# Local attention beside a convolution: softmax divisions moved to GpSimd, one copy per half of the transposed weights, three convolution taps moved off VectorE, both halves scheduled in one group

## The chip, the core and the metric

The kernel runs on one core of a Trainium2 chip, in float32. The metric is device time of one execution in microseconds: 1278.14 us is the median of 3 runs before the change (1277.0 to 1278.47). The profile is of one further execution. PE is TensorE, DVE is VectorE, ACT is ScalarE, POOL is GpSimd; SP issues DMAs.

## The reference, cut to what matters

Three layers follow one another: local attention plus a dynamic convolution, a state-space layer, and a mixture of experts. The change touches the first, on x of shape (2, 256, 48, 48) with 4 heads of 64 channels:

```python
q = (_c1x1(x, Wq, bq) * HD ** (-0.5)).reshape(b * HEAD, HD, n)
k = _c1x1(x, Wk, bk).reshape(b * HEAD, HD, h, w)
v = _c1x1(x, Wv, bv).reshape(b * HEAD, HD, h, w)
uk = _unfold(jnp.pad(k, rpad, mode='reflect'), KA).reshape(b * HEAD, HD, kk, n)   # 7x7 windows
...
att = jnp.einsum('bdn,bdkn->bnk', q, uk + upe[None])
att = jax.nn.softmax(att, axis=-1)
out_att = jnp.einsum('bnk,bdkn->bdn', att, uv).reshape(b, c, h, w)
...
hid = jax.nn.relu(_dwconv(xr, w1))              # depthwise 3x3
oc = _dwconv(hid, w2).reshape(b, kc2, C, h, w)  # depthwise 3x3
...
return rate1 * out_att + rate2 * out_conv
```

Ahead of it stands a group normalisation; the layer's input is added to its output. The kernel adds the convolution's and the attention's part into the tile that holds x.

## The kernel before, in words

Channels lie on partitions, in two halves of 128 (two heads each). The image is cut into blocks of 8 x 16 queries, 18 per batch entry, 36 in all (`block`). The keys that a block can see are 14 x 22 = 308 positions, so its scores are a full 128 x 308 product for each of 4 heads, and a constant mask removes what lies outside a 7 x 7 window. For one half (two heads) of a block:

- `scores` (PE, L776): two products from query tile and key image into a double PSUM bank.
- `least` (DVE, L786): adds the mask, writes the result to the SBUF tile `prob`, and reduces the minimum (queries are scaled by a negative number).
- `exps` (ACT, L797): exponential in place, with the sum read from the accumulator.
- `rden` (DVE, L852): reciprocal of the sums, once per block for all four heads.
- `divide` (ACT, L803): `prob` times the reciprocal, one instruction per head.
- `turn` (PE, L810): six transposes (three pieces of keys for two heads) into a double bank. The pieces are 110, 110 and 88 keys, whole rows of the window.
- `copy` (ACT, L818 and L819): the two long pieces and the short one to the SBUF tile `pt`.
- `mix` (PE, L828): weights times values into a single bank. The values come from a table in HBM by DMA (`val`, SP).
- `add` (DVE, L835): bank plus value bias plus x into x.

The convolution (`convolutions`) works on 8 strips of 24 rows (batch, half, top or bottom). First convolution: tap 4 on ACT (`middle`, L557), taps 1 and 7 as products on ACT into a tile `ct` (L599), added to `hid` by accumulating DMAs that POOL issues (`added`, L603), the other six on DVE (`mac1`, L561). After the ReLU (ACT, L565) the second convolution's nine taps run on DVE (`mac2`, L573), each adding to x in place. Queries (`queries`, L621 and L631), keys (`keys`, with borders copied by POOL at L678 to L685 and a position term by POOL at L654) and values (`values`) are projected as they come due. POOL also scales the next layer's weights in this stage (L428, L449).

The order of instructions is not that of the loops. Each step is given to a planner (`Flow`) with an engine, a cost in ns, what it needs, the buffers it takes and frees, and a due time (`PACE0` per block). Its rank is its due time less the work behind it less a number by kind (`LEAD0`); the planner goes through time and emits, for each free engine, the ready step of lowest rank whose buffers are free. Engines execute in the order emitted, so the planner's costs fix the order, and what really takes longer makes engines wait. POOL's instructions and the DMAs that it issues are kept in that order too. Buffers are counted in `room`: four single and two double PSUM banks, three `prob`, four `pt`, two `ct`, two `hid` and so on.

Of the kernel before, what the change touches and what calls it, by code (L numbers as in the profile page):

```python
# [37 lines left out]
P = 128  # L38
# [3 lines left out]
HD = 64  # L42
# [5 lines left out]
KCH = ((0, 5), (5, 5), (10, 4))  # L48
# [74 lines left out]
class Flow:  # L123
# [8 lines left out]
    def __init__(self, room, lead):  # L132

        self.room, self.lead, self.ops = dict(room), lead, {}
# [8 lines left out]
    @classmethod  # L143
    def kind(cls, key):
        return key if isinstance(key, str) else cls.kind(key[0])

# [3 lines left out]
    def rank(self):  # L150

        after = {k: [] for k in self.ops}
        for k, o in self.ops.items():
            for n in o["needs"]:
                after[n].append(k)
        tail, left = {}, {k: len(after[k]) for k in self.ops}
        ends = [k for k in self.ops if not left[k]]
        for k in ends:
            o = self.ops[k]
            same = [tail[a] for a in after[k] if self.ops[a]["due"] == o["due"]]  # L160
            tail[k] = self.span(o) + max(same, default=0) + self.HOP
            for n in o["needs"]:
                left[n] -= 1
                if not left[n]:
                    ends.append(n)
        return {k: o["due"] - tail[k] - self.lead.get(self.kind(k), 0) for k, o in self.ops.items()}, after
# [62 lines left out]
class Kernel:  # L229
# [49 lines left out]
    def begin_flow(self, pool, room, pace, lead):  # L279

        self.m, self.pace, self.flow, self.tiles, self.last = pool, pace, Flow(room, lead), {}, {}
# [52 lines left out]
    def layer0(self, ctx):  # L334
# [5 lines left out]
        room = dict(bank=4, banks=2, q=2, prob=3, pt=4, val=3, vout=2, hid=2, place=2, ct=2)  # L340
        self.begin_flow(self.pool("att", 1, ctx), room, self.PACE0, self.LEAD0)
        self.kp = [wts.tile([P, HP, HP], F32, name=f"kp{h}") for h in range(NH)]
        self.xp = {(b, h): wts.tile([P, H, W], F32, name=f"xp{b}{h}") for b in range(B) for h in range(NH)}
# [19 lines left out]
    def prepare(self, wts):  # L363
# [15 lines left out]
        for key, cost in (("cst", 9500), ("vec", 9000), ("wp", 8500), ("Wk", 9500), ("Wq", 10500), ("Wv", 11500),  # L379
                          ("win", 22000)):  # L380
            self.arrival((key, 0), cost)
# [7 lines left out]
            new("w2r", NH * 9), v["w2"], r["rate2"], None, ALU.mult), ("vec", 0))  # L389

        self.op(0, ("bv1", 0), "DVE", 220, lambda: vec.tensor_scalar(
            new("bv1", NH), v["bv"], r["rate1"], None, ALU.mult), ("vec", 0))
        self.op(0, ("wv1", 0), "POOL", 1600, lambda: nc.gpsimd.tensor_scalar(
            l0["Wv"], l0["Wv"], r["rate1"], None, ALU.mult), ("vec", 0), ("Wv", 0))
# [63 lines left out]
    def group_norm(self, b):  # L458
# [7 lines left out]
        for h in range(NH):  # L466
# [7 lines left out]
            for i in range(pieces):  # L474
                if i % 2 == 0:
                    self.arrival(("x", (b, h, i // 2)), (4500, 16000)[b] + (i // 2 * NH + h + 1) * 700)
# [50 lines left out]
    def convolutions(self, b):  # L527
# [16 lines left out]
        for n in range(NH * strips):  # L544
# [33 lines left out]
            for k in (1, 7):  # L578
                last = self.added(due, ("1", key, k), rows[0], partial(tap, rows, k=k), hidden, lambda h=h: (self.xp[b, h], 0),
                                  lambda w=w1, k=k: w[:, k : k + 1], before, last)  # L580
            for k in range(9):
                if k != 4 and k not in (1, 7):
# [4 lines left out]
            rest = taps  # L587
            for i, k in enumerate(rest):
                self.op(due, ("c2", (key, k)), "DVE", 1385, partial(mac2, k), *before, uses=[("hid", key)] if i == len(rest) - 1 else [])
                before = [("c2", (key, k))]  # L590

    def added(self, due, key, first, places, out, of, weight, before, last):
# [3 lines left out]
        def product():  # L596
            t = self.large_tile("ct", key, [P, CR + 1, W])
            dst, src = places(o=(t, first), i=of())
            nc.scalar.activation(dst, src, AF.Identity, scale=weight())  # L599

        def issue():
            (dst, _), (t, _) = (places(o=o, i=of()) for o in (out(), (T["ct", key], first)))
            nc.gpsimd.dma_start(dst.rearrange("p r c -> p (r c)"), t.rearrange("p r c -> p (r c)"), accum_op=ALU.add)  # L603

        self.op(due, ("cp", key), "ACT", 1220, product, *before, takes=[("ct", key)])
# [4 lines left out]
    def queries(self, b, rb):  # L610
# [4 lines left out]
        for h in range(NH):  # L615
# [10 lines left out]
            def scale(h=h, key=key):  # L626
                if h == 0:
                    self.large_tile("q", (b, rb), [P, NH, NCB, QR * QC])
                ps = T["bank", ("q", key)][:, : QR * W].rearrange("p (r c) -> p r c", r=QR)
                for cb in range(NCB):  # L630
                    nc.scalar.activation(  # L631
                        T["q", (b, rb)][:, h, cb, :].rearrange("p (r c) -> p r c", r=QR), ps[:, :, cb * QC : (cb + 1) * QC],
                        AF.Identity, bias=l0["bq8"][:, h : h + 1], scale=-(HD ** -0.5),
                    )
# [3 lines left out]
            self.op(c, ("q", key), "ACT", 870, scale, ("qp", key), ("bq8", 0), ("q", (b, rb, 0)) if h else None,  # L638
                    takes=[] if h else [("q", (b, rb))], uses=[("bank", ("q", key))])

    def keys(self, b, g):
# [17 lines left out]
        for h in range(NH):  # L659
# [16 lines left out]
            def border(kp=kp):  # L676
# [4 lines left out]
                for j in range(PAD):  # L681
# [8 lines left out]
                    *[("score", (i, h)) for i in range(old + 1) if b],  # L690
# [64 lines left out]
    def block(self, c):  # L755
# [11 lines left out]
        for h in range(NH):  # L767
            key = (c, h)

            def scores(h=h, key=key):  # L770
                if h == 0:
                    self.large_tile("prob", c, [P, 4, NKEY])
                ps = self.banks_for(("s", key))
                for j in range(2):
# [4 lines left out]
                    )  # L779

# [20 lines left out]
            def divide(h=h):  # L801
                for a in range(2 * h, 2 * h + 2):
                    nc.scalar.mul(T["prob", c][:, a, :], T["prob", c][:, a, :], T["rden", c][:, a : a + 1])  # L803


            def turn(h=h, key=key):
                ps = self.banks_for(("t", key))
                for i, (kr, nr) in enumerate(KCH):
                    for j in range(2):
                        nc.tensor.transpose(  # L810
                            ps[: nr * KC, j, i * P : (i + 1) * P], T["prob", c][:, 2 * h + j, kr * KC : (kr + nr) * KC],
                            self.ident
                        )

            def copy(h=h, key=key):
                full, short = KCH[0][1] * KC, KCH[-1][1] * KC
                pt, ps = self.large_tile("pt", key, [P, 2, len(KCH), P]), T["banks", ("t", key)]
                nc.scalar.copy(pt[:full, :, :2, :].rearrange("p j i q -> p j (i q)"), ps[:full, :, : 2 * P])  # L818
                nc.scalar.copy(pt[:short, :, 2, :], ps[:short, :, 2 * P : 3 * P])  # L819


            def mix(h=h, key=key):
                po = self.bank_for(("o", key))
                for i, (kr, nr) in enumerate(KCH):
                    nk = nr * KC
                    for j in range(2):
                        a = 2 * h + j
                        nc.tensor.matmul(  # L828
                            po[j * HD : (j + 1) * HD, :P], lhsT=T["val", c][:nk, i, a * HD : (a + 1) * HD],
                            rhs=T["pt", key][:nk, j, i, :], start=i == 0, stop=i == len(KCH) - 1,  # L830
                        )

            def add(h=h, key=key):
                x = self.x[b][:, h, :].rearrange("p (r c) -> p r c", r=H)[:, r0 : r0 + QR, c0 : c0 + QC]
                nc.vector.scalar_tensor_tensor(  # L835
                    x, T["bank", ("o", key)][:, :P].rearrange("p (r c) -> p r c", r=QR), self.l0["bv1"][:, h : h + 1],
                    x, ALU.add, ALU.add
                )

            self.op(c, ("score", key), "PE", 512, scores, ("q", (b, rb, h)), *[k for k in rows if k[1][2] == h],  # L840
                    ("score", (c, 0)) if h else None,
                    takes=[("banks", ("s", key))] + ([] if h else [("prob", c)]), mode="rows", uses=[("q", (b, rb))] if last and h == NH - 1 else [])
            self.op(c, ("least", key), "DVE", 950, least, ("score", key), ("cst", 0), ("least", (c, 0)) if h else None,
                    uses=[("banks", ("s", key))])
            self.op(c, ("exps", key), "ACT", 1170, exps, ("least", key), ("exps", (c, 0)) if h else None)
            self.op(c, ("divide", key), "ACT", 990, divide, ("rden", c))
            self.op(c, ("turn", key), "PE", 655, turn, ("divide", key), takes=[("banks", ("t", key))], uses=[("prob", c)])
            self.op(c, ("copy", key), "ACT", 870, copy, ("turn", key), takes=[("pt", key)], uses=[("banks", ("t", key))])
            self.op(c, ("mix", key), "PE", 660, mix, ("copy", key), ("val", c), takes=[("bank", ("o", key))], mode="tiled",
                    uses=[("pt", key)] + ([("val", c)] if h == NH - 1 else []))  # L850
            self.op(c, ("add", key), "DVE", 350, add, ("mix", key), ("bv1", 0), uses=[("bank", ("o", key))])
        self.op(c, ("rden", c), "DVE", 175, lambda: nc.vector.reciprocal(self.small_tile("rden", c, wide), T["den", c]),  # L852
                *[("exps", (c, h)) for h in range(NH)])


        def load():
            val = self.large_tile("val", c, [P, len(KCH), C])
            for i, (kr, nr) in enumerate(KCH):
                nk, first = nr * KC, (r0 + kr) * KC
# [8 lines left out]
        "Wk": -1147950, "Wq": 130187, "Wv": -311640, "add": -66396, "bkp": -1659163, "bq8":  # L868
        487296, "bv1": -67420, "c1": 131452, "c2": -74690, "ca": -343085, "cd": 295831, "copy":
        828342, "cp": -194702, "cst": 1126755, "divide": 116227, "exps": -352759, "ga": 195685,  # L870
        "gneg": 849100, "gs": -87647, "ka": -73324, "kb": -515860, "kk": -132952, "least":
        512500, "line": 1189336, "mix": -72068, "place": -761695, "q": -313065, "qp": -156027,
# [1492 lines left out]
```

## Time and profile before

The profiled execution took 1273.72 us; its span is 1271.9 us.

| engine | busy us in the span | share |
|---|---|---|
| PE | 1210.3 | 95% |
| DVE | 911.8 | 72% |
| ACT | 814.9 | 64% |
| POOL | 574.5 | 45% |

The first layer fills about the first quarter of the span; it is there that DVE and ACT are fullest. In forty slices of 31.8 us:

```profile
PE   4999899997999999999999999999999999999995
...
DVE  6999799997587988789798655655555655556442
ACT  3999899998889888689597653333334343334332
POOL 4723503102267799899889873121212121212220
```

Each digit is a busy share in tenths. A row of groups names line, engine, operation, output and input with their shapes and the count, then the busy time in us and the mean of one in ns, then idle time before the group and who ended it. PE's busy time holds the latency of its pipeline, so a full PE row need not be a full PE.

### The profile page before, as it was taken

The numbers are of one execution on the slowest core, as the hardware profiler recorded it, in microseconds if no ns is written. First come the engines' busy times: TensorE is split into PE (matmuls) and PEld (weight loads), VectorE is DVE, ScalarE is ACT, GpSimd is POOL, SyncE is SP. The second block draws the span as 40 slices with busy tenths as digits, with TensorE's granted clock in tenths as the row PEclk, the third lists the DMA queues.
The fourth block names the chain that finished last, engine by engine and source line by source line (L and its number), as shares of the span: only waits on it lengthen the run. The fifth ranks groups of instructions, "written<-read, shape, count | busy, mean of one in ns | idle before, by whom it ended". The sixth has DMA issues, their size and how long they took to land. (4 is left out here: it accounts for less than half of the span.)

```text
span 1271.9 us, 23413 instructions
## 1 busy us (share of the span) xinstructions
PE 1210.3 (95%) x7952; PEld 966.5 (76%) x7952; DVE 911.8 (72%) x2401; ACT 814.9 (64%) x1978; POOL 574.5 (45%) x781
## 2 busy tenths in 40 slices
PE   4999899997999999999999999999999999999995
PEld 2666566655567777777777888999999999999994
DVE  6999799997587988789798655655555655556442
ACT  3999899998889888689597653333334343334332
POOL 4723503102267799899889873121212121212220
PEclk9999899999899999999999999999999999999998
DMA  8553537241223334334545139667658667656756
GB/s 280 148 148 99 136 113 167 86 106 31 74 87 95 108 99 121 124 103 148 164 144 177 59 134 292 196 229 230 214 171 258 190 229 222 225 172 223 221 177 212
DMA packets 103961, 203.74 MB, mean 160 GB/s; under 512 B 10891, under 2 KB 82908, under 8 KB 98908
## 3 DMA queue, kind: packets, MB, share of 16 engines
q1 hardware_dynamic: 85020, 168.51, 38.5%
q0 software_dynamic: 16704, 29.37, 12.0%
q10 hardware_dynamic: 2116, 4.33, 1.0%
q8 instruction: 65, 1.06, 0.3%
q14 instruction: 56, 0.46, 0.1%
HBM read 154.24 MB, written 43.23 MB: 155 GB/s over the span
## 5 line engine op out<-in xcount | busy, mean ns | idle before, releaser
L2094 POOL DMA_INDIRECT acc<-ey,token x70 | 109.3, 1562 | 367.6 <-ACT ey L2093 324.7
L2088 ACT ACTIVATE hid<-bank,bt 128x256 f32<-128x256 f32 (+1 forms) x288 | 132.0, 460 | 171.0 <-PE bank L2084 166.6
L2084 PE MATMUL bank<-ext,wt 128*128 128x256 f32 (+1 forms) x1152 | 241.3, 368 | 0.0
L2084 PEld LDWEIGHTS bank<-ext,wt 128*128 128x128 f32 x1152 | 207.6, 191 | 24.4
L573 DVE SCALAR_TENSOR_TENSOR x<-hid,w2r,x 128x1128 f32<-128x1128 f32 (+3 forms) x72 | 99.5, 1391 | 4.7 <-ACT hid L565 4.0
L2127 PE MATMUL po<-ts,ss 128*128 128x128 f32 x768 | 96.3, 275 | 0.0
L915 PE MATMUL bank<-xn,win 128*128 128x387 f32 x240 | 92.9, 511 | 2.1 <-ACT t L998 2.1
L1128 DVE SCALAR_TENSOR_TENSOR xc<-bank,vec,xc 128x384 f32<-128x384 f32 x144 | 86.6, 609 | 8.4 <-ACT xc L1117 8.1
L2127 PEld LDWEIGHTS po<-ts,ss 128*128 128x128 f32 x768 | 90.9, 192 | 0.0
L1344 ACT ACTIVATE mt<-mt,cum 128x128 f32<-128x128 f32 x288 | 87.7, 393 | 0.0
L2131 ACT COPY u<-po 128x128 f32<-128x128 f32 x32 | 8.5, 265 | 114.3 <-PE po L2127 114.3
L1678 POOL DMA_INDIRECT xs<-u,rows x72 | 73.3, 1018 | 17.5 <-issue 14.9
L797 ACT ACTIVATE prob<-prob,top 128x308 f32<-128x308 f32 x144 | 79.1, 570 | 0.4 <-DVE top L786 0.4
L1450 PE MATMUL bank<-wout,y 128*128 128x264 f32 x288 | 73.4, 402 | 0.1
L2071 DVE TENSOR_TENSOR ss<-hid 128x512 f32<-128x512 f32 x32 | 22.1, 691 | 70.6 <-ACT hid L2088 70.6
L915 PE MATMUL zbank<-xn,win 128*128 128x384 f32 x192 | 71.2, 493 | 0.0
L803 ACT ACTIVATE prob<-prob,rden 128x308 f32<-128x308 f32 x144 | 68.9, 567 | 1.0 <-DVE rden L852 0.7
L561 DVE SCALAR_TENSOR_TENSOR hid<-xp,vec,hid 128x1175 f32<-128x1175 f32 (+1 forms) x48 | 69.3, 1443 | 0.1
L810 PE MATMUL banks<-cst,prob 128*110 128x128 f32 (+1 forms) x432 | 60.9, 282 | 8.8 <-ACT pt L819 4.1
L810 PEld LDWEIGHTS banks<-cst,prob 128*110 128x110 f32 (+1 forms) x432 | 47.3, 132 | 27.9 <-ACT prob L803 6.9
L786 DVE CUSTOM_DVE_ANT_0 prob<-banks,cst 128x308 f32<-128x308 f32 x144 | 62.0, 471 | 8.9 <-PE banks L776 8.4
L603 POOL DMA_DIRECT2D hid<-ct x16 | 14.1, 884 | 116.3 <-ACT hid L557 88.5
(333 smaller groups left out, 2999.1 us busy)
## 6 DMA issues: line engine op xcount, KB each, us to landing
wt<-in_We SPq DMA_DIRECT2D x36, 2048.0 KB
mt<-decays SPq DMA_DIRECT2D x36, 512.0 KB
ex<-xs SPq DMA_DIRECT2D x36, 265.0 KB
rd<-decays SPq DMA_DIRECT2D x68, 128.0 KB
val<-vtab SPq DMA_DIRECT2D x72, 110.0 KB
bt<-in_We SPq DMA_DIRECT2D x36, 136.0 KB
hid<-ct POOLq DMA_DIRECT2D x8, 600.0 KB, 5.5
hid<-ct POOLq DMA_DIRECT2D x8, 576.0 KB, 5.4
```

Of the source, the lines that this page charges most:

```text
L573: nc.vector.scalar_tensor_tensor(dst, src, w[:, k : k + 1], dst, ALU.mult, ALU.add)
L797: nc.scalar.activation(t, t, AF.Exp, bias=T["top", c][:, a : a + 1], scale=-1.0, accum_out=T["den", c][:, a : a + 1])
L810: nc.tensor.transpose(ps[: nr * KC, j, i * P : (i + 1) * P], T["prob", c][:, 2 * h + j, kr * KC : (kr + nr) * KC], self.ident)
L915: self.nc.tensor.matmul(ps, lhsT=lhs(k), rhs=rhs(k), start=k == 0, stop=k == NH - 1)
L1128: nc.vector.scalar_tensor_tensor(out(), T["bank", ("cv", at)][:, i : i + TB], wc[:, i : i + 1], out(), ALU.mult, ALU.add)
L1344: nc.scalar.activation(t, t, AF.Relu, bias=at_s, scale=-1.0)
L1450: nc.tensor.matmul(ps[:, : C + E], lhsT=T["y", c][:, m, :], rhs=self.l1["wout"][:, m, :], start=m == 0, stop=m == NZ - 1,)
L1678: ins = nc.gpsimd.indirect_dma_start(self.xs, bass.IndirectOffsetOnAxis(ap=of("rows")[:, i, q : q + 1], axis=0), T["u2", g][:, i, :], None,)
L2084: nc.tensor.matmul(ps[:, :rows], lhsT=w1[:, k, c * P : (c + 1) * P], rhs=xt[:, k, :], start=k == 0, stop=k == NH - 1,)
L2088: nc.scalar.activation(hid[:, c, :], ps[:, :rows], AF.Gelu, bias=bt[:, c : c + 1])
L2094: put = nc.gpsimd.indirect_dma_start(self.acc, bass.IndirectOffsetOnAxis(ap=token[:, j : j + 1], axis=0), y, None, compute_op=ALU.add)
L2127: nc.tensor.matmul(p[name], lhsT=v[a][:, c], rhs=v[w][:, c], start=c == 0, stop=c == NHC // 2 - 1)
```

## The change

All of it is in the first layer, but for one new pool of small tiles opened behind it (`self.small = self.pool("small1", 4)`).

- Divisions: the second half of every block and, in every third block, the first half too are scaled by GpSimd (`nc.gpsimd.tensor_scalar`); the rest stay on ACT. The reciprocal is taken per half.
- Pieces of keys: three of nearly equal length (102, 103, 103), so that one ACT copy moves all three.
- Second convolution: tap 4 goes to ACT, into a tile `cg` together with the value bias; taps 1 and 7 go to ACT products and accumulating DMAs into `cg`; DVE adds `cg` to x once per strip and keeps six taps. In the first convolution the DMA taps now come behind the DVE taps, except in the first strip.
- One group: scores of both halves are one planner step, and so are both weighted sums, which share one bank and are added by one DVE instruction.
- Query scaling: one ACT instruction for three blocks instead of three.
- Planner: single banks 4 to 2, double banks 2 to 3, `prob` 3 to 4, two `cg`; leads kept apart for the first and the second batch entry and set anew; arrival times of inputs set later.

```diff
-KCH = ((0, 5), (5, 5), (10, 4))
+KW = -(-NKEY // 3)
+KCH = ((0, NKEY - 2 * KW), (NKEY - 2 * KW, KW), (NKEY - KW, KW))
...
-        room = dict(bank=4, banks=2, q=2, prob=3, pt=4, val=3, vout=2, hid=2, place=2, ct=2)
+        room = dict(bank=2, banks=3, q=2, prob=4, pt=4, val=3, vout=2, hid=2, place=2, ct=2, cg=2)
...
+            before = [last]
+            for k in sorted(set(range(9)) - {4}, key=lambda k: (k in (1, 7)) == (key[:2] == (0, 0))):
+                if k in (1, 7):
+                    last = self.added(due, ("1", key, k), rows, partial(tap, rows, k=k), hidden,
...
-            rest = taps
+            rest = [k for k in taps if k not in (4, 1, 7)]
+            def centre(h=h, top=top, key=key, hidden=hidden):
+                g = self.large_tile("cg", key, [P, CR, W])
+                dst, src = tap((top, top + CR), (g, top), hidden(), 4)
+                nc.scalar.activation(
+                    dst, src, AF.Identity, bias=self.l0["bv1"][:, h : h + 1],
+                    scale=self.l0["w2r"][:, 9 * h + 4 : 9 * h + 5]
+                )
+            def gather(key=key, strip=strip):
+                nc.vector.tensor_add(strip(), strip(), T["cg", key])
+            self.op(due, ("g2", (key, 4)), "ACT", 1200, centre, *before, ("bv1", 0), takes=[("cg", key)], uses=[("hid", key)])
+            last = ("g2", (key, 4))
+            for k in (4, 1, 7):
+                if k != 4:
+                    last = self.added(due, ("2", key, k), (top, top + CR), partial(tap, (top, top + CR), k=k),
+                                      lambda key=key, top=top: (T["cg", key], top), hidden,
...
+            self.op(due, ("c3", key), "DVE", 1290, gather, summed, *before, uses=[("cg", key)])
...
-                for cb in range(NCB):
-                    nc.scalar.activation(
-                        T["q", (b, rb)][:, h, cb, :].rearrange("p (r c) -> p r c", r=QR), ps[:, :, cb * QC : (cb + 1) * QC],
-                        AF.Identity, bias=l0["bq8"][:, h : h + 1], scale=-(HD ** -0.5),
-                    )
+                nc.scalar.activation(
+                    T["q", (b, rb)][:, h].rearrange("p b (r c) -> p b r c", r=QR),
+                    T["bank", ("q", key)][:, : QR * W].rearrange("p (r b c) -> p b r c", r=QR, b=NCB),
+                    AF.Identity, bias=l0["bq8"][:, h : h + 1], scale=-(HD ** -0.5),
+                )
...
+            def inverse(h=h):
+                if ("rden", c) not in T:
+                    self.small_tile("rden", c, wide)
+                part = slice(2 * h, 2 * h + 2)
+                nc.vector.reciprocal(T["rden", c][:, part], T["den", c][:, part])
...
+            def divide(engine, h=h):
                 for a in range(2 * h, 2 * h + 2):
-                    nc.scalar.mul(T["prob", c][:, a, :], T["prob", c][:, a, :], T["rden", c][:, a : a + 1])
+                    t, r = T["prob", c][:, a, :], T["rden", c][:, a : a + 1]
+                    if engine == "ACT":
+                        nc.scalar.mul(t, t, r)
+                    else:
+                        nc.gpsimd.tensor_scalar(t, t, r, None, ALU.mult)
...
-                nc.scalar.copy(pt[:full, :, :2, :].rearrange("p j i q -> p j (i q)"), ps[:full, :, : 2 * P])
-                nc.scalar.copy(pt[:short, :, 2, :], ps[:short, :, 2 * P : 3 * P])
+                nc.scalar.copy(pt[:KW].rearrange("p j i q -> p j (i q)"), ps[:KW, :, : len(KCH) * P])
...
+            engine = "POOL" if h == 1 or c % 3 == 0 else "ACT"
+            self.op(c, ("divide" if engine == "ACT" else "scale", key), engine, 990 if engine == "ACT" else 2650,
+                    partial(divide, engine), ("rden", key))
...
+        self.op(c, ("mix", c), "PE", 1320, mix, *[("copy", (c, h)) for h in range(NH)], ("val", c), takes=[("bank", ("o", c))],
+                mode="tiled", uses=[*[("pt", (c, h)) for h in range(NH)], ("val", c)])
+        def add():
+            x = self.x[b].rearrange("p h (r c) -> p h r c", r=H)[:, :, r0 : r0 + QR, c0 : c0 + QC]
+            po = T["bank", ("o", c)][:, : NH * P].rearrange("p (h r c) -> p h r c", h=NH, r=QR)
+            nc.vector.tensor_add(x, x, po)
```

## The prediction on record

> **What bounds the kernel now.** The whole page says PE 95% busy, but that mixes stages, and its chain that ended last covers only the final 20 us. The change touches the first layer alone (convolution and local attention), so I read the busy times by windows. The edges come from the timeline: the first normalised input is written from 18.3 us on, and the last attention sum ends at 305.75 us, where the next layer's first transposes start.
>
> ```profile
> core 0: us, PE busy (x) PEld busy (x) DVE busy (x) ACT busy (x) POOL busy (x), PEclk, DMA share, GB/s
> ...
> 64.00:128.00 64.00, 61.27 (x451) 39.88 (x449) 62.80 (x128) 62.03 (x172) 17.92 (x45) 1.00 0.45 124
> ...
> 144.00:160.00 16.00, 11.81 (x87) 7.58 (x87) 9.46 (x28) 11.20 (x31) 4.16 (x7) 0.79 0.52 116
> ...
> 18.30:305.75 287.45, 271.83 (x1936) 178.60 (x1936) 268.39 (x566) 268.15 (x706) 83.45 (x178) 0.98 0.47 125
> ```
>
> Read the last row first: in this stage of 287.45 us DVE is busy for 268.4 and ACT for 268.2, both 93%, and both reach 97% in the long windows such as 64 to 128. They bound it together; to shorten the stage both must lose work. POOL does 83.5 and is the free engine. PE's 272 is padded: six transposes alone take 0.84 us and twelve in a row 1.47, so a half block costs PE 0.63, not 0.84; with such steps 72 half blocks of 0.52 + 0.63 + 0.66 us (scores, transposes, weighted sum) need 130 us, and the projections at most the 106 us of their rows: under 240 in all. Two hollow places remain: 144 to 160 us, where ACT stood 4.2 us before a `ct` buffer because an accumulating DMA had not landed, and the tail after 288 us.
>
> The groups by shape, stage rows (count, busy us, mean ns):
>
> ```profile
> L803 ACT ACTIVATE prob<-prob,rden 128x308 f32<-128x308 f32 x144 | 68.9, 567 | 1.0 <-DVE rden L852 0.7
> ...
> L573 DVE SCALAR_TENSOR_TENSOR x<-hid,w2r,x 128x1128 f32<-128x1128 f32 x32 | 44.4, 1388 | 0.2
> L818 ACT COPY pt<-banks 110x512 f32<-110x512 f32 x72 | 42.7, 593 | 6.0 <-PE banks L810 5.1 <-PE bank L828 0.4
> ...
> L819 ACT COPY pt<-banks 88x256 f32<-88x256 f32 x72 | 28.0, 388 | 0.0
> ...
> L835 DVE SCALAR_TENSOR_TENSOR x<-bank,bv,x 128x128 f32<-128x128 f32 x72 | 23.7, 342 | 2.3 <-PE bank L828 1.9
> ```
>
> Consecutive ACT instructions overlap by about 0.09 us and DVE's by 0.08, so I price by what an instruction adds to busy time.
>
> **ACT.** Of 144 divisions 96 go to GpSimd. Four in a row take 1.88 us, 0.47 each: 96 x 0.47 = 45 off. The two copies of a half (0.593 + 0.388, less overlaps 0.80) become one of 768 columns; 256 more columns cost 0.205 us, so 0.593 + 0.205 - 0.09 = 0.71: 72 x 0.09 = 6 off. Three query scalings (72 are 21.0 us busy, so 3 x 0.29) become one of 384 columns; a copy of that size (L1084) takes 0.47, an activation with a bias (L1117) 0.66, and I take 0.57 less 0.09: 24 x 0.4 = 9 off. Added: 8 centre taps and 16 more products, each like the `ct` products of 1.27 us, 24 x 1.18 = 28. Net: 45 + 6 + 9 - 28 = 32 off, ACT 268 to 236. It stops being a bound.
>
> **DVE.** Of 72 second-convolution taps 24 go; the stage's 72 take 99.45 us, 1.38 each: 33.1 off. Added are 8 gathers of 128x1152 from SBUF. Additions of 512 columns (L2070) take 0.69 us, of 1024 (L1352) 1.215, hence 1.35: 10.8 on. The 72 output sums (23.7) become 36 of 256 columns, like an existing sum of that size (L1482: 0.48, less overlap 0.41): 36 x 0.41 = 15, 9 off. 36 reciprocals more at 0.09 to 0.17: 4 on. Net 27 off: 241. The row for the gather is an extrapolation by an eighth, so its error is below 1 us.
>
> **GpSimd.** The changed program's list of instructions holds 96 scalings of 128x308 on POOL, 32 accumulating DMAs instead of 16, and, behind the stage, the same order on all five engines. No row shows a POOL scaling of 308 columns. The one of 256 (L449) takes 0.92 us undisturbed (shortest of four), the one of 512 (L393) 1.60; in between 1.06. But POOL and DVE disturb each other:
>
> ```profile
> 42.96 1.88 POOL L428 TENSOR_SCALAR win<-win,vec 128x640 f32<-128x640 f32 x1
> ...
> 43.23 3.14 DVE L561 SCALAR_TENSOR_TENSOR hid<-xp,vec,hid 128x1128 f32<-128x1128 f32 x2
> ```
>
> ```profile
> 52.04 2.49 POOL L449 TENSOR_SCALAR wout<-wout,vec 128x256 f32<-128x256 f32 x2
> ...
> 52.08 1.67 DVE L561 SCALAR_TENSOR_TENSOR hid<-xp,vec,hid 128x1175 f32<-128x1175 f32 x1
> ...
> 55.16 4.19 DVE L573 SCALAR_TENSOR_TENSOR x<-hid,w2r,x 128x1152 f32<-128x1152 f32 x3
> ...
> 56.70 1.31 POOL L678 COPY kp<-kp 128x10 f32<-128x10 f32 x1
> ```
>
> A ten-column copy, 0.20 us when free, lasts 1.31 when issued into a tap: POOL waits until the tap is over. The other way round DVE loses less: the tap at 52.08, begun behind a 256-column scaling, takes 1.67 instead of 1.43, and the two at 43.23, begun into one of 640 columns, 3.14 instead of 2.7. That is 0.24 and 0.44, as if POOL held DVE only while it reads; for 308 columns I put 0.27.
>
> The Trainium skill ("SBUF — State Buffer", "Who interferes with whom" and the section on the two sides above it) states a rule that speaks against this change: a GpSimd instruction and a DVE instruction with two SBUF inputs take a shared port pair as an exclusive lock for the whole instruction. POOL's waits here fit it; DVE's do not, since 1.88 us of POOL cost a tap 0.44. By the rule DVE would lose up to 96 x 0.55 x 1.06 = 56 us, and the stage would end some 30 us later than before.
>
> Taps and gathers are 96 x 1.4 + 8 x 1.35 = 145 us of DVE's 241, so a POOL reading meets one with a chance of 0.55 to 0.6. DVE's loss: none at best (readings beside work that reads PSUM), 96 x 0.27 = 26 if each hits, and 56 if the whole instruction holds it. I take 96 x 0.55 x 0.27 = 14, nearest to the rows. DVE: 241 + 14 = 255.
>
> A POOL scaling waits for half a tap (0.69) in 0.55 of the cases, 1.06 + 0.38 = 1.44; bounds 1.06 and 1.06 + 1.38 = 2.44. POOL: 83.5 + 96 x 1.44 + 16 x 0.86 (a DMA issue's median) = 235 us, bounds 199 and 331. It covers its work, but barely, in a stage of 270.
>
> The new waits: a half block's transposes now follow reciprocal and POOL instead of reciprocal and ACT, 2.9 us instead of 0.95. Behind them on PE stand other blocks' scores and products; four `prob` tiles instead of three give them room. PSUM is recut (two single banks, three double), which one group for scores and one for the weighted sum need; that can hold PE, whose 240 us leave 30 spare. The 16 added DMAs cost POOL the issues above; each lands 4.8 to 7.7 us later (L603's landings), and three behind one another (product, DMA, DMA, gather) stand beside six taps, 8 us, and other blocks.
>
> **The sum.** DVE is the bound with 255. Before, DVE filled 93.4% of the stage next to an equally full ACT; with ACT at 236 I take 94%: 255 / 0.94 = 271, which is 16 less than 287.45. Start, seam and tail stay inside that share; the tail stays serial, with the last four half blocks' scalings in one row on POOL (4 x 2.1 us). The profiled execution took 1273.7 us (span 1271.9); less 16 it is 1258. It lay 4.4 below the median of 1278.1; on the median I forecast 1262.
>
> **Rivals.**
> 1. DVE loses nothing to POOL: 241 / 0.94 = 256, 31 less, 1247. For it: the minimum with the mask (L786, 144 of 0.47 us) reads PSUM, and POOL's copies beside it stay at 0.2 us. Against: taps follow one another. Chance 0.17.
> 2. POOL becomes the bound, the slower side. It executes in order, scalings queue behind DMA issues that wait for an earlier DMA, and PE, ACT and DVE wait for the scalings. In the profile before, those issues waited 25 us for landings. The stage is longer than now if 83.5 + 13.8 + 25 + 96 s exceeds 287, that is from s = 1.72 us per scaling on. At 1.85: 300 us, 12 more, 1290. For it: most scalings follow a reciprocal, behind which DVE likes to start a tap, and the second of a pair meets the next tap. Against: a scaling that stands ahead of a DMA issue fills time that POOL now spends waiting. Chance 0.18.
> 3. DVE is held for the whole POOL instruction (the 56 us above): (241 + 56) / 0.94 = 316, 1307. The two rows above contradict it. Chance 0.03.
> 4. The work goes, and new waits eat it: twice as many `ct` products, each of which can hold ACT as the one at 151 us did (about 5 us for all engines), and two single banks. Two such stops more, 10 us: 1262 + 10, 1272. Chance 0.15.
> That the change does not do what it says is excluded by the counts above.
>
> **Numbers.** Forecast 1262 (1253 to 1270), chance 0.47; the rivals as given. Range 1245 to 1286: it leaves out rival 3, half of rival 2 and the edge of rival 1. A measurement of this kernel tells 0.2% (2.6 us) from no change. Faster: 0.47 + 0.17 + most of rival 4 = 0.75. Same 0.07: rival 4 with a third or fourth stop, and rival 2 near its turning point. Slower 0.18.
>
> **What would show it.** Right: stage end near 289 us instead of 306; DVE 250 to 260 us busy up to there, ACT near 236, POOL 220 to 250; scalings of 1.2 to 1.7 us; taps beside them lengthened by about 0.3. Wrong: scalings above 1.75 us and PE waiting for POOL (rival 2); taps of 2.4 us beside scalings (rival 3); idle ACT before `ct` (rival 4); a later layer that is not the same length as before.

## The result, and the profile after

The changed kernel takes 1531.43 us (median of 4 runs, 1528.0 to 1532.38) beside 1278.31 for the kernel before in the same job (4 runs, 1277.0 to 1282.81): ratio 1.197, 95% interval [1.193, 1.200]. The prediction had 1262 with a range of 1245 to 1286. It is wrong in sign, and by 269 us in size.

Where the 253 us lie is quickly found. The last attention sum ends at 560.3 us instead of 305.75; what follows it takes 970.0 us of the span instead of 966.15. The first layer has become 255 us longer. The forty slices, 38.3 us each now:

```profile
PE   4755376546575549999999999989999999999996
...
DVE  7733274434453416888888898546555555565552
ACT  2734283535373428988878887623343333433333
POOL 5823172325353323678989989851222222222221
PEclk9967697767786759999999999999999999999998
```

In the first fourteen slices no engine is full, and TensorE's granted clock has fallen too. The stage by windows (columns as in the prediction):

```profile
18.30:560.30 542.00, 324.22 (x1936) 223.54 (x1935) 243.34 (x548) 244.70 (x513) 222.38 (x291) 0.75 0.33 83
```

The work did go as planned: DVE 243 us (268 before), ACT 245 (268), GpSimd 222 (83). PE's 324 us belong to the same 1936 products as the 272 before; with the clock at 0.75 and gaps between them, each counts for more. With 542 us to fill, all of this is under 60%. Such a stage may well wait for something that is no engine. The groups of the stage by shape:

```profile
L853 POOL TENSOR_SCALAR prob<-prob,rden 128x308 f32<-128x308 f32 x96 | 140.6, 1646 | 191.1 <-DVE rden L845 176.6 <-PE banks L810 14.4
...
L865 ACT COPY pt<-banks 103x768 f32<-103x768 f32 x72 | 55.9, 798 | 91.2 <-PE banks L859 55.5 <-PE bank L885 35.5
...
L577 DVE SCALAR_TENSOR_TENSOR x<-hid,w2r,x 128x1128 f32<-128x1128 f32 x32 | 46.0, 1438 | 0.5
...
L896 DVE TENSOR_TENSOR x<-x,bank 128x256 f32<-128x256 f32 x36 | 15.1, 419 | 185.5 <-PE bank L885 185.3
```

Busy times and means are about as planned; the idle times before the groups (third part) are new. The output sums (L896) take 15 us, and DVE stands still before them for 185. The waits (engine, line, releaser: us in all, times, longest; PEld is TensorE's loading of weights):

```profile
DVE x L896 <- PE bank L885: 185.3, 26, 17.2
POOL prob L853 <- DVE rden L845: 176.6, 16, 32.0
PEld bank L885 <- DMA val<-vtab: 159.3, 40, 9.9
PE bank L885 <- DMA val<-vtab: 156.4, 40, 9.6
ACT vout L755 <- DMA vraster<-vout: 83.4, 4, 24.4
```

Read from the bottom up: the first two rows are engines waiting for engines, which explains nothing yet; in the last three a DMA is late. L885 is the weighted sum, `val` its values from HBM. Its wait (156 us) and that of the value projection for its own copy to HBM (83 us, same SP queue) make 240 us, about the 255 that are missing, though the two may overlap in part. In the stage of the kernel before, neither wait shows at all.

A stretch of the timeline with the loads (start, duration, engine, line, operation, tile, count, idle time before and releaser):

```profile
500.91 0.44 PE L885 MATMUL bank<-pt,val 103*64 103x128 f32 x4 [0.34 <-DMA val<-vtab]
505.45 2.04 PE L885 MATMUL bank<-pt,val 103*64 103x128 f32 x20 [4.10 <-DMA val<-vtab]
510.91 0.70 PE L885 MATMUL bank<-pt,val 103*64 103x128 f32 x4 [3.42 <-DMA val<-vtab]
515.43 1.97 PE L885 MATMUL bank<-pt,val 103*64 103x128 f32 x16 [3.82 <-DMA val<-vtab]
```

and what the DMA engines moved from 500 to 530 us, in slices of 0.75 us:

```profile
DMA  2300000000000131000000000013100599910010
GB/s 55 101 31 23 23 23 22 23 23 23 22 23 23 41 108 36 23 23 23 22 23 23 23 22 23 23 40 83 61 23 23 112 198 235 241 33 15 15 36 13
```

PE starts a new piece every 4.5 us, and between them the chip moves a steady 23 GB/s with 16 DMA engines almost idle (0 tenths). 103 KB in 4.5 us are 23 GB/s: one load is under way, on what looks like one engine of 16. SP, which issues the loads, is now held by most of the issues themselves (SPq is SP's queue of instructions; duration in ns: least, median, longest). The first row is from the kernel after, the second from the kernel before:

```profile
L904 SPq DMA_DIRECT2D val<-vtab x108: 260/4435/9547, 64.4 to 543.0; - x108
```

```profile
L860 SPq DMA_DIRECT2D val<-vtab x108: 282/356/1645, 62.3 to 294.2; - x108
```

Added up, these 108 issues hold SP for 354 us (48 before), most of the stage of 542, and the value projection's copies to HBM are issued by SP in between. The two long loads of a block, at 4.5 us each, need 330 us for 36 blocks; how the rest of the 542 is made up was not taken apart.

The long loads carry fewer bytes than before, 103 KB instead of 110. What changed is the number of partitions, 103 instead of 110. The Trainium skill ("DMA: Bandwidth & Descriptors", "Why a DMA increments its semaphore by 16 and not by 1") states that a transfer is spread over the largest number of engines up to 16 that divides the size of the slowest dimension on both its sides. By that rule 110 rows go to 11 engines, 88 to 11, 102 to 6, and 103, a prime, to one. The trace agrees with one engine for 103. The same page ("Specifications") gives about 27 GiB/s for an engine, which is 29 GB/s. Here 23 GB/s were measured, and the measurement decides.

### The profile page after: what moved, and what is told of

It reads as the page before. It is cut to its first block, busy times and chain, and to the rows that moved or that the text cites. A ratio compares the mean times of both kernels' runs of the same rounds, so it can differ in the third digit from the quotient of the medians.

```text
span 1530.3 us, 23342 instructions
## 1 busy us (share of the span) xinstructions
PE 1263.7 (83%) x7952; PEld 1011.5 (66%) x7952; DVE 890.8 (58%) x2385; ACT 793.3 (52%) x1786; POOL 713.5 (47%) x893
## 5 line engine op out<-in xcount | busy, mean ns | idle before, releaser
L853 POOL TENSOR_SCALAR prob<-prob,rden 128x308 f32<-128x308 f32 x96 | 140.6, 1646 | 191.1 <-DVE rden L845 176.6
L885 PE MATMUL bank<-pt,val 103*64 103x128 f32 (+1 forms) x864 | 87.7, 354 | 157.8 <-DMA val<-vtab 156.4
L885 PEld LDWEIGHTS bank<-pt,val 103*64 103x64 f32 (+1 forms) x864 | 63.7, 178 | 179.4 <-DMA val<-vtab 159.3
L896 DVE TENSOR_TENSOR x<-x,bank 128x256 f32<-128x256 f32 x36 | 15.1, 419 | 185.5 <-PE bank L885 185.3
L865 ACT COPY pt<-banks 103x768 f32<-103x768 f32 x72 | 55.9, 798 | 91.2 <-PE banks L859 55.5
L859 PE MATMUL banks<-cst,prob 128*103 128x128 f32 x432 | 72.0, 320 | 25.7 <-ACT pt L865 21.4
L859 PEld LDWEIGHTS banks<-cst,prob 128*103 128x103 f32 x432 | 63.0, 203 | 42.5 <-ACT pt L865 21.3
L810 PE MATMUL banks<-kp,q 64*128 64x308 f32 x288 | 58.2, 526 | 19.2 <-ACT pt L865 16.1
L1501 PE MATMUL bank<-wout,y 128*128 128x264 f32 x288 | 70.3, 389 | 0.1
```

The lines of the kernel that those rows point to most:

```text
L853: nc.gpsimd.tensor_scalar(t, t, r, None, ALU.mult)
L859: nc.tensor.transpose(ps[:KW, j, i * P : (i + 1) * P], T["prob", c][:, 2 * h + j, k0 : k0 + KW], self.ident)
L885: nc.tensor.matmul(po[j * HD : (j + 1) * HD, h * P : (h + 1) * P], lhsT=T["val", c][:nk, i, a * HD : (a + 1) * HD], rhs=T["pt", (c, h)][:n ...
```

## The experiments

Theory: the 103-row loads are slow, whatever else the change does. Rivals: the recut of the PSUM banks, GpSimd's scalings, or the added accumulating DMAs make the stage long and the loads only look late. Unless a diff says otherwise it is against the changed kernel. "Stage end" is the end of the last attention sum in one profile. Among versions whose ratios to the kernel before agree within 0.2% it differs by 4.7 us (305.6 to 310.3), so differences of 2 us in it mean little.

**Rows that divide well.** `p104`, pieces 100, 104 and 104, the order of the engines' instructions as in the changed kernel:

```diff
-KW = -(-NKEY // 3)
+KW = 104
```

> The changed kernel with pieces of 100, 104 and 104 keys instead of 102, 103 and 103; nothing else differs, the order on PE, DVE, ACT and POOL is the same. Theory 1: a load of 103 partitions of values moves on very few DMA engines, because 103 has no divisor but itself; in the changed kernel 72 such loads, one behind another, take 72 x 7.5 us, the 541 us of its first stage (18 to 560 us). With 104 = 8 x 13 and 100 = 10 x 10 the loads spread: PE no longer waits for val (156 us before), the stage ends near 290 us and the kernel takes 1250 to 1285 us. The Trainium skill (DMA: Bandwidth & Descriptors, on how many engines a DMA gets) states that the largest divisor up to 16 of the slowest dimension sets the number of engines; by it 103 gives one engine and 104 thirteen. Theory 2: the new order of work asks for the values too late, or their three buffers come free too late, whatever the shape: 1500 us or more, with PE still waiting over 130 us for val.

Measured: 1275.76 us, ratio to the kernel before 0.9993 [0.998, 1.001]; stage end 308.3. One row more in the two long loads takes back the whole loss. What is left of PE's wait for `val`:

```profile
PEld bank L885 <- DMA val<-vtab: 3.6, 2, 3.4
```

But the gain that was forecast is not there either. The 7.5 us that the expectation gives a load are the stage divided by 72; the trace shows 4.5.

**The same pieces, the load cut.** `cut96` keeps 102, 103 and 103 and issues each load in two:

```diff
-                nc.sync.dma_start(val[:nk, i, :], self.vtab[b, cb, first : first + nk, :])
+                for p0, p1 in ((0, 96), (96, nk)): nc.sync.dma_start(val[p0:p1, i, :], self.vtab[b, cb, first + p0 : first + p1, :])
```

> The changed kernel, pieces of 102, 103 and 103 keys kept everywhere, but each load of values is issued as two: 96 partitions and the remaining 6 or 7. Order on PE, DVE, ACT and POOL unchanged; SP issues 108 loads more at about 0.3 us each, beside other work. Theory 1 (shape of the load): 1250 to 1290 us, PE's wait for val under 20 us. Theory 2 (order or buffers): 1500 us or more.

Measured: 1276.49, ratio 1.0005 [0.998, 1.003]; stage end 310.3. Products, transposes and copies still have 103 rows here, so it is the transfer's shape that costs, not theirs.

**The pieces alone.** `before103` is the kernel before with nothing but the three new pieces (its two copies of a half block remain; the loops take the pieces' new bounds):

```diff
-KCH = ((0, 5), (5, 5), (10, 4))
+KW = -(-NKEY // 3)
+KCH = ((0, NKEY - 2 * KW), (NKEY - 2 * KW, KW), (NKEY - KW, KW))
```

> The kernel before with only the pieces of keys changed, from 110, 110 and 88 to 102, 103 and 103 (loads, transposes, copies, weighted sums); two copies per half, divisions on ACT and all the rest as before, in the same order. Theory 1: the loads alone make it slow, 72 loads of 103 partitions at 7.5 us, so the stage ends near 560 us and the kernel takes 1480 to 1540 us. Theory 2: no change, 1270 to 1290 us.

Measured: 1480.01, ratio 1.159 [1.155, 1.162]; stage end 509.7. The stage ends 50 us sooner than expected, because the 7.5 us per load were too many. But there is no scaling on GpSimd, no new bank and no added DMA, and 204 us of the loss are there. PE's wait for the values in `before103`:

```profile
PE bank L828 <- DMA val<-vtab: 142.1, 40, 11.4
```

The rivals named above fall with it as causes of these 204 us, and `p104` and `cut96`, which keep all that they name, leave them next to nothing of the other 50.

**Two engines, and odd rows.** `p106` (96, 106, 106; 106 is 2 x 53) and `p105` (98, 105, 105; odd, but 15 divides it):

```diff
-KW = -(-NKEY // 3)
+KW = 106
```

> The changed kernel with pieces of 96, 106 and 106 keys: 106 = 2 x 53. Theory 1, as a dose: with two engines a load of 106 KB takes half of 7.5 us, about 3.9; 72 of them need 280 us, about as long as the rest of the stage, so the kernel takes 1265 to 1340 us, with PE still waiting for val some 10 to 60 us, clearly more than with 104. Theory 2: 1500 us or more. A third possibility, that any piece off a whole window row (22 keys) makes the loads slow because of alignment in HBM, gives 1500 us here and with 104.

```diff
-KW = -(-NKEY // 3)
+KW = 105
```

> The changed kernel with pieces of 98, 105 and 105 keys. Theory (a load is spread over as many DMA engines as the largest divisor up to 16 of its partitions, 14 and 15 here): the loads land as with 104, the stage ends at 306 to 311 us, 1274 to 1280 in all. Rival (odd counts, or counts that are no multiple of four or eight, are what makes a load slow, whatever they divide by): loads as with 103 or 106, stage end 380 us or later, over 1345 in all. In the trace: PE's wait for the values below 6 us (theory) or above 30 (rival).

Measured: 106 gives 1350.71, ratio 1.060 [1.056, 1.064], stage end 382.0, some 10 us above the top of what was expected; 105 gives 1275.83, ratio 1.0003 [0.999, 1.002], stage end 306.1. Odd is harmless, and even does not help. Nor is it the start off a whole window row in HBM, the third possibility of the expectation: 104 and 105 are off it too. The clearest rows are the load of the DMA engines in `p106` from 320 to 350 us (tenths) and what they moved:

```profile
DMA  0020548999411111111151111132211111111321
GB/s 0 0 60 30 171 116 162 187 227 222 102 55 33 30 24 29 38 46 49 48 163 46 45 46 45 46 137 68 68 45 46 45 46 45 57 45 46 132 74 45
```

46 GB/s where 103 rows gave 23, at a share of one tenth where 103 rows had none: twice one engine. The waits of `p106`:

```profile
PEld bank L885 <- DMA val<-vtab: 35.7, 15, 5.3
PE bank L885 <- DMA val<-vtab: 32.6, 13, 5.0
ACT vout L755 <- DMA vraster<-vout: 28.8, 4, 12.7
```

Two loads in a block need 2 x 106 KB at 46 GB/s, 4.7 us, 170 us for 36 blocks, less than the stage. They still cost 74 us over `p104`, so the rate alone does not explain it. The value projection's own transfers come late as well (last row), and blocks may come unevenly. That these transfers stand behind the loads in SP's queue is argued from the rows (SP's longest issue of such a copy is 0.4 us in the kernel before, 7.2 in the changed one and 7.9 here); no run here separates it.

**Why the repaired kernel gains nothing.** In `p104` the work sums are near the forecast and the stage is not. The window up to 308.2 us, and the main waits, both of `p104`:

```profile
18.30:308.20 289.90, 265.45 (x1936) 185.50 (x1934) 245.98 (x547) 242.35 (x513) 234.05 (x290) 0.96 0.64 155
```

```profile
POOL prob L853 <- DVE rden L845: 29.1, 8, 6.6
...
PEld banks L859 <- POOL prob L853: 12.3, 14, 2.0
...
PE banks L859 <- POOL prob L853: 9.0, 9, 1.8
...
ACT ct L626 <- DMA hid<-ct: 5.2, 3, 2.7
```

DVE is at 246 of 290, 85% full instead of 94. Two suspects show: transposes (L859) that wait for GpSimd, and the accumulating DMAs, with a DMA share of 0.64 instead of 0.47. Three kernels of `p104` take them away in the same order of instructions. `thin_pool` scales 2 of 308 columns of each row, so that most weights stay undivided:

```diff
-                        nc.gpsimd.tensor_scalar(t, t, r, None, ALU.mult)
+                        nc.gpsimd.tensor_scalar(t[:, :2], t[:, :2], r, None, ALU.mult)
```

> The changed kernel with pieces of 100, 104 and 104 keys, in the same order on every engine, but each of the 96 GpSimd scalings covers 2 of its 308 columns: the division of the other 306 columns of those heads is left out. With healed loads the stage ends at 308 us instead of the 289 forecast, though DVE (246 us), ACT (242) and POOL (234) have the work that was forecast. Theory A: GpSimd holds it, by its time (1.5 us per scaling, 3.0 per half block, in order with key borders and DMA issues) and by lengthening taps: without it the stage ends at 285 to 292 us, the kernel takes 1252 to 1262 us, POOL's scalings fall from 145 to 20 us and DVE from 246 to about 239. Theory B: the accumulating DMAs hold ACT, DVE and POOL: less than 4 us here. Theory C: the emitted order and the recut PSUM hold it: less than 4 us here.

`thin_dma` accumulates one image row instead of all, so that two taps of each convolution are nearly left out:

```diff
-            nc.gpsimd.dma_start(to, of, accum_op=ALU.add)
+            nc.gpsimd.dma_start(to[:, :W], of[:, :W], accum_op=ALU.add)
```

> The same kernel (100, 104, 104; same order, full scalings), but each of the 32 accumulating DMAs adds one row of 48 columns instead of 23 to 25 rows: most of the taps 1 and 7 of both convolutions is left out of the sum. Theory A (GpSimd's scalings): within 4 us of 1276. Theory B (landings of 4.7 to 9.0 us hold ACT, DVE and POOL): 8 us or more faster, under 1268. Theory C: within 4 us.

`thin_both` has both edits.

> Both: scalings of 2 columns and accumulating DMAs of one row, same order; the left-out parts are those of the two runs before. If A and B each hold part, the gains add up. Theory C, order and banks: still over 1270 us. Theory A alone: as with thin scalings, 1252 to 1262.

Measured, in all: 1305.04 (ratio 1.021 [1.018, 1.024]), 1309.91 (1.025 [1.022, 1.028]), 1297.82 (1.015 [1.012, 1.018]). The totals that were expected can't be used: the later layers now get other data, and the mixture of experts runs more work for it (160 products at L2163 instead of 96), so what follows the stage takes 1008 to 1010 us in the three instead of 972. So the reading goes by the stage end: 295.4, 300.1 and 288.5, against 308.3. That is 13 us for GpSimd's scaling time, 8 for the accumulating DMAs, 20 for both. The profile of `p104` is of an execution 6 us above its median; against the 305.6 to 306.1 of `p112` and `p105` below, it is about 10, 6 and 17. `thin_pool` misses what was expected of its stage end: 295.4 lies between theory A (285 to 292) and the others (304 or later). Its scalings still take 74.5 us instead of 20, so not all of GpSimd's part is taken away. DVE's work also falls by 5 us (241.1 instead of 246.0), which is in the 13.

`thin_both` ends the stage where the forecast put it (289), but not for the forecast's reason: DVE is busy for 241 of 270 us, 89% and not 94, with less work than the 255 forecast. What holds the other five per cent was not tried. GpSimd's groups (busy us, mean ns, idle time before), of `p104` and then of `thin_pool`:

```profile
L853 POOL TENSOR_SCALAR prob<-prob,rden 128x308 f32<-128x308 f32 x96 | 144.8, 1626 | 30.0 <-DVE rden L845 29.1 <-PE banks L859 0.7
```

```profile
L853 POOL TENSOR_SCALAR prob<-prob,rden 128x2 f32<-128x2 f32 x96 | 74.5, 838 | 56.8 <-DVE rden L845 45.6 <-PE bank L885 7.1 <-PE banks L810 2.5
```

**Fewer scalings on GpSimd.** `half_pool` (of `p104`) gives it the second halves alone, with the planner told so:

```diff
-            engine = "POOL" if h == 1 or c % 3 == 0 else "ACT"
+            engine = "POOL" if h == 1 else "ACT"
```

> The same kernel (100, 104, 104), whole computation, but GpSimd scales only the second half of every block: 72 scalings instead of 96, 24 more divisions on ACT (11 us: 242 to 253). The planner makes a new order. Theory A: POOL is relieved by 36 us and ACT still fits, 1264 to 1273 us. Theories B and C: 1274 us or more, as ACT gains work and nothing else goes.

Measured: 1300.46, ratio 1.018 [1.012, 1.023]; stage end 327.7. It was worse, but the planner had written another order, with new waits (ACT 14.2 us for the value projection's transfer, GpSimd 15 to 16 each for two kinds of products), so it told nothing of the scalings. The next three keep the order of `p104`. `p112` has pieces 84, 112 and 112; `keep72` is `p112` with the planner's view kept and only the instruction issued on ACT; `keep72t` does the same for the last three blocks' second halves.

```diff
-KW = -(-NKEY // 3)
+KW = 112
```

> The changed kernel with pieces of 84, 112 and 112 keys (14, 16 and 16 engines if the largest divisor decides; 104 has 13). Theory (what is left of the stage is GpSimd's scaling chain and the accumulating DMAs, not the value loads): same as with 104 within 3 us, stage end 305 to 311, 1273 to 1279. Rival (the value loads on 13 of 16 engines still load some DMA engines unevenly and delay the accumulating DMAs): ct landings below those of 104 (4.7 to 9.0 us), stage end 300 to 304, 1268 to 1272, which would beat both kernels.

```diff
-                    if engine == "ACT":
+                    if engine == "ACT" or h == 0:
```

> The kernel with pieces of 84, 112 and 112 keys, its steps issued in the same order, but the 24 scalings of first halves that GpSimd did are now ACT's, issued at the same place; GpSimd keeps 72. Only this moves. Theory (GpSimd's scaling chain holds the stage, by 13 us for 96 scalings): GpSimd busy 198 instead of 234, ACT 253 instead of 242, the stage ends 2 to 4 us earlier, 302 to 304, 1270 to 1273 beside a kernel before of 1276. Rival (what half_pool lost came from taking 24 scalings back to ACT and not from its new order): the stage ends at 315 or later, 1285 or more.

```diff
-                    if engine == "ACT":
+                    if engine == "ACT" or h == 0 or c > 32:
```

> The same, and the last three blocks' second halves scaled on ACT as well, in the stage's tail, where the chain is serial. Theory (in the tail each half block waits for two scalings of 1.1 to 1.7 us on GpSimd, 0.95 for both on ACT): another 1 to 4 us earlier than with 72 alone, stage end 299 to 303, 1267 to 1272, the first version below both kernels. Rival (the tail waits for PE's transposes and copies, whoever scales): no earlier than with 72 alone, within 1 us.

| kernel | us | ratio to before [95%] | stage end | GpSimd, ACT busy to 305.6 |
|---|---|---|---|---|
| p112 | 1273.46 | 0.9993 [0.998, 1.001] | 305.6 | 234, 243 |
| keep72 | 1273.39 | 0.9972 [0.995, 0.999] | 303.7 | 202, 253 |
| keep72t | 1275.58 | 0.9994 [0.998, 1.001] | 303.4 | 196, 256 |

`p112` can't be told from `p104`. `keep72` is the one version whose interval lies below the kernel before, by 0.3%, though it overlaps with that of `p112`; its stage ends 2 us earlier, as expected, but one profile hardly tells so little. PE's wait for the scalings, in `p112` and then in `keep72`, shows the intended effect:

```profile
PEld banks L859 <- POOL prob L853: 13.4, 17, 2.0
...
PE banks L859 <- POOL prob L853: 9.0, 10, 1.8
```

```profile
PEld banks L859 <- POOL prob L853: 3.8, 7, 1.4
...
PE banks L859 <- POOL prob L853: 1.8, 3, 1.2
```

Seven us less of PE's wait go with 2 us less of stage. `keep72t` ends its stage within 0.3 us of `keep72`, as the rival in its expectation said: who scales in the tail does not move it. Its median lies 2.2 us above that of `keep72`, more than the scatter of the twelve runs of each explains, and no profile here shows where. The loss of `half_pool` was thus the order, not the split: the same 72 scalings on GpSimd end at 327.7 or, in the order of `p112`, at 303.7.

## Why the prediction was wrong, point by point

- **The step that failed: the price of the pieces.** The prediction priced them as one ACT copy instead of two, 6 us off, and counted of the DMAs "32 accumulating DMAs instead of 16". The 108 value loads, whose row count the same edit changes, stand in no sentence, so that their change was put at nothing without a reason. What stood in its place: a load of 103 rows moves at 23 GB/s and takes 4.5 us. `before103` prices this at 204 us of stage in the kernel before, `cut96` at 250 in the changed one. No rival had this mechanism, and rivals 2 and 3, the slower ones, are not what happened.
- **ACT 236**: 242 in `p104`. 26 us off instead of 32; the copy took 0.796 us (0.80 by the prediction's working, 0.71 after overlap), the query scaling 0.577 (0.57).
- **DVE 255**: 246. The gather was right (1.352 us for 1.35). The loss to GpSimd was about a third of what was put: with scalings of 2 columns DVE has 241.1, with full ones 246.0, 5 us instead of 14; the 1128-column tap of L577 goes from 1.444 to 1.480 us. Rival 3, the whole instruction held, falls: it asked for 56.
- **GpSimd 235**: 234; 1.51 us per scaling for 1.44. The turning point of rival 2 (1.72) was not reached, and its sum still missed that GpSimd need not be full to hold the stage.
- **Fill of 94%** (the share of the stage in which DVE is busy): the mis-sized term of what remains. It was taken from a kernel in which a half block went reciprocal, ACT, transpose. With GpSimd in between it is 85%: 246 / 0.85 = 290 instead of 255 / 0.94 = 271. The runs give 10 to 13 us of the longer stage to the scalings' time and 6 to 8 to the accumulating DMAs; with both thin the fill is still 89%. So without the loads' fault rival 4 (1272, "the work goes, and new waits eat it") would have been nearest: 1273 to 1276.
- **The seam and the later layers** were as put: 970 us behind the stage for 966.

What is left open: how the 74 us of `p106`, and the 255 of the changed kernel, divide between late values and late value copies; what keeps the fill at 89% with thin scalings and thin DMAs; and why 7 us less of PE's wait for GpSimd give only 2 us of stage.

## What to carry to other kernels

Where a change alters a tile's partition count, price its DMAs as well as its instructions: reckon how many engines the new count is spread over, and take a count with a large divisor up to 16 (here 104, 105 or 112), not a large prime such as 103. When all engines are half empty and a DMA ends the waits, look at GB/s in quiet slices: a steady small figure, here 23 or 46, can be one or two engines at work. And when work moves from a full engine to an empty one, don't keep the old fill: a longer chain between two engines can cost even where neither of them is full.

## What the runs showed of the hardware that was not expected

- A load of 103 rows of 1 KB runs at 23 GB/s, one of 106 rows at 46; with 104, 105 or 112 rows PE waits for the values under 4 us in all. While the slow loads are under way, the instruction that issues a value load holds SP for 4.4 us in the median, instead of 0.36.
- A scaling of two columns on GpSimd takes 0.28 us at least, but 0.84 on average in this stage (`thin_pool`); one of 308 columns takes 1.04 at least and 1.63 on average (`p104`). So either mean lies 0.56 to 0.58 us above the shortest.
- The same 1936 products were 324 us of PE time at a granted clock of 0.75 and 265 at 0.96.
